# Band attention layers: the mask added to the scores by VectorE instead of by mask products on TensorE

## The chip, the core and the metric

The kernel runs on one core of a Trainium2 chip. The time is device time in microseconds of one execution; the shown time is the median of the runs. PE is TensorE (matmuls), PEld its weight loads, DVE VectorE, ACT ScalarE, POOL GpSimd, and SP the engine that issues most DMAs.

## The reference

The reference is a decoder with layer norms ahead of each part: a tensor x of 32 batch elements, 128 positions and 128 features goes through self-attention, cross-attention and feed-forward parts, eleven of them, and a last part named `L3_ffn`. The change lies in this last part. It holds six layers; each is a local attention with 16 heads of 64 features and a gated feed-forward:

```python
def local_attention(q, k, v):                      # windows of w = 32 positions
    ...                                            # keys and values of the window before and its own
    mask = (it < jb) | (it > jb + w) | (jb == -1)
    sim = jnp.einsum('bhwie,bhwje->bhwij', bq, bk2) * QK_SCALE      # 8.0
    sim = jnp.where(mask, -jnp.finfo(sim.dtype).max, sim)
    attn = jax.nn.softmax(sim, -1)
    out = jnp.einsum('bhwij,bhwje->bhwie', attn, bv2)
def attn_layer(x, Wqkv, qs, ksc, Wo):
    q, k, v = jnp.split(x @ Wqkv, 3, -1)           # then by heads
    q = l2norm(q) * qs
    k = l2norm(k) * ksc
    q = q * cos * scale + rotate_half(q) * sin * scale
    k = k * cos * inv + rotate_half(k) * sin * inv
    out = local_attention(q, k, v)
    return out @ Wo                                # 1024 features to 128
def ffn_layer(x, g, bln, W1, b1, W2, b2):
    hg = layer_norm(x, g, bln) @ W1 + b1
    a, gate = jnp.split(hg, 2, -1)
    return a * gelu(gate) @ W2 + b2
for i in range(6):
    x = attn_layer(shift_tokens(x), ...) + x
    x = ffn_layer(shift_tokens(x), ...) + x
```

A query at position i sees the keys at positions j with i - 32 <= j <= i: a band below the diagonal.

## The kernel before

The first 2770 us of the program are the other parts, which the change touches only through one constant tile. The last part is the method `l3_ffn` of class `Fast`. X, the stream Z and all work of a layer stay in SBUF; only the weights of the next layer are fetched while the present one runs.

**Work.** One unit of work n is one batch element in one layer: 6 x 32 = 192 units. The kernel doesn't cut the sequence into windows. It computes, for each head, the whole 128 x 128 matrix of scores, transposed (keys on partitions, queries along the free dimension), adds a mask of 0 inside the band and -1e30 outside, and takes the exponential, with no maximum subtracted since q and k are normalized. The sum of the exponentials comes out of the product with the values, through a column of ones in `va`.

**Steps of a unit**, with the tiles that they write:
- `queries(n, w)`: two products of 512 columns (the profile shows two rows for each fp32 product) into `qk`, 16 heads of 64 features; w=0 gives the queries, w=1 the keys.
- `squares`: ACT squares `qk` into `sq`. `swapped` and `rotated`: DVE multiplies `qk` by the two rotary tables `tab` into `rt` and `raw`; POOL adds them.
- `summed` and `scaled`: DVE sums the squares by head into `ss` and begins the inverse root; POOL finishes it and scales `raw`.
- `turned(n, us)`: TensorE transposes `raw` in four batches u=0..3 of four 128 x 128 tiles each into `rT`; ACT copies u=0 and 2, DVE u=1 and 3, into `qkT`.
- `scores(n)`: into two tiles `sc`, of eight heads each: first four mask products (an identity times `bandT`, 512 columns each, bfloat16), then 16 score products that add to them; ACT takes the exponential, scale 8, into `P`.
- `values`: the products of `P` with `va` into `av`; DVE takes the reciprocal of the sums `rs` and multiplies into `ao`. `features`: TensorE transposes `ao` (`oTp`), ACT copies to `oT`. `projected`: the product with `wo` into `y`, added to Z by DVE. `valued`: the product `vp` and its copy to `va`.
- Steps named `ff_...` and `shifted` work on four units at a time: the gated feed-forward (`gp`, `ap`, `u`, `fy`) and the shift of positions (`zT`, `zs`).

**Order.** The order is written out by hand. A loop over t runs a fixed list of steps, each for the unit t minus a lag:

```python
steps = ((features, 5), (summed, 1, 1), (scaled, 1), (queries, 0, 0), (squares, 0), (swapped, 0, 0),
         (rotated, 0, 0), (turned, 2, (0, 1)), (scores, 3), (summed, 0, 0), (turned, 2, (2, 3)),
         (queries, 0, 1), (squares, 0), (swapped, 0, 1), (rotated, 0, 1), (projected, 5), (values, 4))
blocks = ((ff_normed, 7), (ff_turn, 8), (ff_down, 11), (ff_up, 10), (ff_gates, 9), (ff_norm, 6))
```

The classes `Ordered` and `Lane` keep every engine to this order: each instruction of TensorE, VectorE, ScalarE and GpSimd is issued after the one before it on its engine. Each engine then runs ahead of the others only as far as its waits allow. Because all these instructions are recorded by `Lane`, the profile gives one line for them (L1342), and they are told apart by their tiles.

**PSUM.** Two pools share the eight banks. `p2` (function `banks`) has three buffers of two banks, used in turn by `qk`, `sc`, `sc`, `qk`, `av`, `av`, `vp`. `p1` (function `bank`) has two buffers of one bank, for `rT`, `oTp`, `y` and all small results. A tile that takes a buffer waits until the tile that had it before has been read.

Of the kernel before, what the change touches and what calls it, by code (L numbers as in the profile page):

```python
# [13 lines left out]
F32 = mybir.dt.float32  # L14
BF16 = mybir.dt.bfloat16
# [3 lines left out]
ALU = mybir.AluOpType  # L19
# [238 lines left out]
class General:  # L258
    def __init__(self, ctx, tc, i, out, names):
        self.tc, self.nc, self.i, self.out = tc, tc.nc, i, out  # L260
        nc = self.nc
        mats, cols, rows = names
        self.mat_at = {n: j for j, n in enumerate(mats)}
        self.col_at = {n: j for j, n in enumerate(cols)}
        self.row_at = {n: j for j, n in enumerate(rows)}
        cp = self.cp = ctx.enter_context(tc.tile_pool(name="const", bufs=1))
        self.X = cp.tile([128, NB, 128], F32, name="X")
        self.load_x()

        def load(key, dt=F32, eng=None):  # L270
            src = i[key]
            t = cp.tile(list(src.shape), dt, name=key)
            (eng or nc.scalar).dma_start(out=t, in_=src)
            return t

        self.half = load("c_half", BF16)
        self.small = load("c_small")
        self.cols = load("cols")
        self.rows = load("rows")
        self.big = load("c_big")  # L280
        self.ident = cp.tile([128, 128], F32, name="ident")
        make_identity(nc, self.ident)
        self.identh = cp.tile([128, 2, 128], BF16, name="identh")
        nc.vector.tensor_copy(self.identh[:, 0, :], self.ident)
        nc.vector.tensor_scalar(self.identh[:, 1, :], self.ident, 80.0, None, ALU.mult)
        self.ones = cp.tile([1, 128], F32, name="ones")
        nc.vector.memset(self.ones, 1.0)
        self.eps = cp.tile([128, 1], F32, name="eps")
        nc.vector.memset(self.eps, EPS)
        self.mv = cp.tile([128, NB, 2], F32, name="mv")  # L290
        self.rstd = cp.tile([128, NB], F32, name="rstd")
# [225 lines left out]
    def l0_ffn(self):  # L517
        nc, tc = self.nc, self.tc
        scale = 128.0 ** -0.5
        with ExitStack() as es:  # L520
            wk = es.enter_context(tc.tile_pool(name="L0f", bufs=2))
            one = es.enter_context(tc.tile_pool(name="L0f1", bufs=1))
            Z = one.tile([128, NB, 128], F32, name="Z")
            ss = one.tile([128, NB], F32, name="ss")
            self.rstds()
            for b4 in range(NB // 4):
# [18 lines left out]
                for j in range(4):  # L545
# [29 lines left out]
                    self.mm(y, aoT, self.mat("L0f_o"))  # L575
                    nc.vector.tensor_copy(Z[:, b, :], y)
                    self.sumsq(wk, ss[:, b:b + 1], y)
            self.l2scale(ss)
            ss2 = one.tile([128, NB], F32, name="ss2")
            for b4 in range(NB // 4):  # L580
                zT = self.trans4(wk, self.scaled4(wk, Z, ss, b4), "zT")
                for j in range(4):
                    b = 4 * b4 + j
                    y = self.p1([128, 128], "y")
                    self.mm(y, zT[:, 128 * j:128 * j + 128], self.mat("L0f_ff"))
                    nc.vector.tensor_copy(Z[:, b, :], y)
                    self.sumsq(wk, ss2[:, b:b + 1], y)
            self.l2scale(ss2)
            for b4 in range(NB // 4):
                z = self.scaled4(wk, Z, ss2, b4)  # L590
                nc.scalar.activation(z, z, AF.Gelu)
# [13 lines left out]

    def scaled4(self, wk, Z, ss, b4):
        z = wk.tile([128, 4, 128], F32, tag="zs", name="zs")
        for j in range(4):
            b = 4 * b4 + j
            self.nc.vector.tensor_scalar(z[:, j, :], Z[:, b, :], ss[:, b:b + 1], None, ALU.mult)  # L610
        return z
# [747 lines left out]
class Fast(General):  # L1359
# [6 lines left out]
    def __init__(self, *a):  # L1366
        super().__init__(*a)
        nc, cp = self.nc, self.cp
        self.cert = cp.tile([128, 2, 16], F32, name="cert")
        nc.vector.memset(self.cert, 1.0)  # L1370

        self.bandT = cp.tile([128, 4, 128], BF16, name="bandT")
        nc.gpsimd.memset(self.bandT, 0.0)
        for sign, base in ((1, 0), (-1, 32)):
            nc.gpsimd.affine_select(out=self.bandT, in_=self.bandT, pattern=[[0, 4], [sign, 128]],
                                    compare_op=ALU.is_ge, fill=-1.0e30, base=base, channel_multiplier=-sign)
        self.bandT = self.bandT.rearrange("p c q -> p (c q)")
        self.ncert = 0

    def all(self):  # L1380
# [428 lines left out]
    def l3_ffn(self):  # L1809
# [3 lines left out]
        nc = self.nc = Ordered(plain, tc)  # L1813
        N = DEPTH * NB
        with ExitStack() as es:
            one = es.enter_context(tc.tile_pool(name="L3f1", bufs=1))
# [4 lines left out]
            def mm(out, lhsT, rhs, start=True, stop=True):  # L1821
                nc.tensor.matmul(out, lhsT=lhsT, rhs=rhs, start=start, stop=stop)
# [7 lines left out]
            def banks(shape, name):  # L1830
                return p2.tile(shape, F32, tag="b", name=name)

            rot = one.tile([128, 256], F32, name="rot")
            nc.sync.dma_start(out=rot, in_=i["c_rot"].rearrange("s w c d -> s (w c d)"))
            Z = one.tile([128, NB, 128], F32, name="Z")
            zs2 = [one.tile([128, 4, 128], F32, name=f"zs{j}") for j in range(2)]
            va2 = [one.tile([128, 16, 65], F32, name=f"va{j}") for j in range(2)]
# [180 lines left out]
            def scores(n):  # L2018
                s = S[n]
                qkT = s["qkT"]  # L2020

                sc = [banks([128, 2, 4, 128], "sc") for _ in range(2)]
                for f in range(2):
                    for e in range(2):
                        mm(sc[f][:, e].rearrange("p c q -> p (c q)"), self.identh[:, 0, :], self.bandT, stop=False)
                s["P"] = []
                for f in range(2):
                    for c in range(4):
                        for e in range(2):
                            r = slice(64 * e, 64 * e + 64)  # L2030
                            mm(sc[f][:, e, c, :], qkT[r, 8 + 4 * f + c, :], qkT[r, 4 * f + c, :], start=False, stop=c == 3)
                    P = wk.tile([128, 8, 128], F32, tag="P", name="P", bufs=4)
                    nc.scalar.activation(P.rearrange("p h q -> p (h q)"), sc[f].rearrange("p e c q -> p (e c q)"), AF.Exp,
                                         scale=8.0)
                    s["P"].append(P)
# [96 lines left out]
            def ff_down(g):  # L2132
# [10 lines left out]
                if l == DEPTH - 1:  # L2143
# [4 lines left out]
            ahead = ((normed, 3), (x_values, 5), (x_scores, 6), (x_keys, 7), (x_turn, 8), (x_norm, 9), (x_root, 10))  # L2148
# [4 lines that stand above are left out]
# [906 lines left out]
```

## Time and profile before

| | us |
|---|---|
| median of 3 runs (lowest to highest) | 6221.49 (6221.09 to 6223.54) |
| the profiled execution | 6220.55 |
| its span, from the first to the last instruction | 6218.8 |
| busy in the span: PE | 5581.7 (90%) |
| PEld | 3944.6 (63%) |
| DVE | 4045.7 (65%) |
| POOL | 3086.2 (50%) |
| ACT | 2985.2 (48%) |
| mask products `sc<-bandT`: 768 rows of 0.379 (192 x 4) | first at 2806.5, last at 6158.6 |
| exponentials `P<-sc`: 384 rows, mean 1.022 | 372.4 |

The shares are averages over the whole program; the band layers fill the time from about 2770 to the end, and only they hold the instructions that change. Times of rows are microseconds from the span's start. A matmul's row is longer than the distance to the next one's start, because matmuls overlap; what a batch of them takes on PE is read from start to start.

### The profile page before, as it was taken

How to read it: one execution, taken by the hardware profiler on the slowest of the kernel's cores; microseconds unless marked ns; L12 is line 12 of the kernel's file. 1: busy time of each engine (PE TensorE's matmuls, PEld its weight loads, DVE VectorE, ACT ScalarE, POOL GpSimd, SP SyncE). 2: the span in 40 equal slices, each digit the busy share in tenths (PEclk: the TensorE clock that was granted, in tenths of full speed). 3: DMA queues.
4: the chain of work that ended last, by engine and by line, in shares of the span. 5: the costliest groups of instructions: out<-in, count | busy, mean ns of one | idle time of the engine just before them, and what ended most of it. 6: DMA issues, size and time to landing. Idle time of an engine off the chain costs nothing.

```text
span 6218.8 us, 137908 instructions
## 1 busy us (share of the span) xinstructions
PE 5581.7 (90%) x56611; PEld 3944.6 (63%) x56611; DVE 4045.7 (65%) x11609; ACT 2985.2 (48%) x4283; POOL 3086.2 (50%) x4833
## 2 busy tenths in 40 slices
PE   8967967777869999869999999999999999999998
PEld 4534546754546666646667767777777777766775
DVE  5576532345539999957666666666666676667664
ACT  5656621114425555524555545555555555554553
POOL 0041011011015555537666666666766667666773
PEclk9988976769989999989999999999999999999999
DMA  1000046543012222210000000000000000000000
GB/s 42 2 1 1 2 169 239 170 143 104 7 23 53 52 55 50 52 35 5 5 17 11 8 1 1 15 5 1 12 8 1 1 15 5 1 1 1 1 1 15
DMA packets 243263, 207.46 MB, mean 33 GB/s; under 512 B 125650, under 2 KB 230457, under 8 KB 237502
## 3 DMA queue, kind: packets, MB, share of 16 engines
q1 hardware_dynamic: 239164, 161.93, 9.1%
q0 software_dynamic: 2304, 33.56, 1.4%
q8 instruction: 447, 7.32, 0.5%
q10 hardware_dynamic: 1154, 3.06, 0.1%
q14 instruction: 194, 1.59, 0.1%
HBM read 140.57 MB, written 57.93 MB: 32 GB/s over the span
## 4 chain that ended last, share of the span: by engine, by line
PE 54%; DVE 10%; ACT 3%; issue 1%; POOL 1%; DMA 1%; SPq 1%; ACTq 0%; DVEq 0%; POOLq 0%
PE qk L1342 11%; PE sc L1342 8%; PE rT L1342 6%; PE vp L1342 6%; PE av L1342 5%; PE y L1342 5%; PE gp L1342 3%; PE oTp L1342 3%; PE fy L1342 2%; DVE rt L1342 1%; DVE raw L1342 1%; DVE ao L1342 1%; DVE neg L1342 1%; ACT sq L1342 1%; PE tp L1342 1%
## 5 line engine op out<-in xcount | busy, mean ns | idle before, releaser
L1342 POOL TENSOR_TENSOR raw<-raw,rt 128x1024 f32<-128x1024 f32 x384 | 902.9, 2357 | 335.9 <-DVE raw L1342 335.7
L1342 DVE TENSOR_TENSOR rt<-qk,tab 128x1024 f32<-128x1024 f32 x384 | 470.2, 1224 | 881.4 <-ACT sq L1342 862.4
L1342 POOL TENSOR_TENSOR raw<-raw,ry 128x2048 f32<-128x2048 f32 x224 | 811.3, 3622 | 17.6
L1342 PE MATMUL qk<-wqkv,zs 128*128 128x512 f32 x1536 | 727.6, 597 | 3.0 <-DVE zs L1342 3.0
L1342 ACT ACTIVATE sq<-qk 128x1024 f32<-128x1024 f32 x448 | 459.2, 1025 | 465.8 <-PE qk L1342 334.5
L1342 POOL TENSOR_TENSOR rt<-ry 128x32 f32<-128x32 f32 (+1 forms) x864 | 198.4, 230 | 751.1 <-DVE ry L1342 642.6
L1342 DVE TENSOR_REDUCE ss<-sq 128x16 f32<-128x1024 f32 x448 | 539.0, 1208 | 48.4 <-ACT sq L1342 47.1
L1342 DVE TENSOR_TENSOR raw<-qk,tab 128x1024 f32<-128x1024 f32 x384 | 466.1, 1214 | 0.0
L1342 ACT ACTIVATE P<-sc 128x1024 f32<-128x1024 f32 x384 | 372.4, 1022 | 187.7 <-PE sc L1342 187.2
L1342 ACT ACTIVATE PT<-sc 128x1024 f32<-128x1024 f32 x384 | 372.6, 1025 | 168.8 <-PE sc L1342 168.3
L1342 PEld LDWEIGHTS rT<-ident,raw 128*128 128x128 f32 x3072 | 342.0, 141 | 164.9 <-issue 65.8
L1342 PE MATMUL rT<-ident,raw 128*128 128x128 f32 x3072 | 433.5, 280 | 14.4 <-POOL raw L1342 6.1
L1342 ACT COPY va<-vp 128x1024 f32<-128x1024 f32 (+1 forms) x232 | 218.2, 941 | 453.3 <-PE vp L1342 453.1
L1342 PEld LDWEIGHTS y<-wo,oT 128*128 128x128 f32 x3072 | 372.8, 192 | 91.5 <-issue 78.7
L1342 PEld LDWEIGHTS sc<-qkT 64*128 64x128 f32 x6144 | 357.9, 188 | 81.4 <-issue 81.4
L1342 PE MATMUL av<-va,P 128*64 128x65 f32 x12288 | 400.9, 223 | 0.0
L1342 PE MATMUL sc<-qkT 64*128 64x128 f32 x6144 | 394.6, 278 | 0.0
L1342 PEld LDWEIGHTS av<-va,P 128*64 128x64 f32 x12288 | 374.3, 137 | 23.8 <-issue 0.8
L1342 PEld LDWEIGHTS qk<-wqkv,zs 128*128 128x128 f32 x1536 | 264.2, 192 | 192.1 <-issue 188.3
L1342 PE MATMUL y<-wo,oT 128*128 128x128 f32 x3072 | 374.4, 275 | 1.4 <-DVE qkT L1342 0.8
L1342 PE MATMUL vp<-wqkv,zs 128*128 128x512 f32 x768 | 362.9, 595 | 0.7 <-DVE rs L1342 0.7
L1342 POOL TENSOR_TENSOR X<-X,brep 128x512 f32<-128x512 f32 x24 | 30.5, 1271 | 548.5 <-DVE xn L1342 548.5
(425 smaller groups left out, 11609.2 us busy)
## 6 DMA issues: line engine op xcount, KB each, us to landing
rows<-scr SPq DMA_DIRECT2D x32, 672.0 KB
tup<-whole SPq DMA_DIRECT2D x8, 2048.0 KB
gt<-tup SPq DMA_DIRECT2D x64, 256.0 KB
tdn<-whole SPq DMA_DIRECT2D x8, 2048.0 KB
gd<-tdn SPq DMA_DIRECT2D x128, 128.0 KB
T<-flt SPq DMA_DIRECT2D x16, 1024.0 KB
wqkv<-in_dqkv SPq DMA_DIRECT2D x6, 1536.0 KB
scr<-dots SPq DMA_DIRECT2D x128, 66.0 KB
```

The costliest lines, as they stand in the source:

```text
L1342: self.last = call(*a, **k)
```

## The change

The mask moves from TensorE to VectorE. The constant `bandT` (bfloat16, 128 x 512, built at the program's start) and the four mask products of each unit go. A new constant `band` (fp32, 128 x 128) is built at the start of `l3_ffn`. The score products now write `sc` with nothing beneath them, all 16 of a unit first. Then, for each of the two halves, VectorE adds `band`, repeated for eight heads, to the 128 x 1024 scores in place in PSUM, and ScalarE's exponential follows.

```diff
-        self.bandT = cp.tile([128, 4, 128], BF16, name="bandT")
-        nc.gpsimd.memset(self.bandT, 0.0)
-        for sign, base in ((1, 0), (-1, 32)):
-            nc.gpsimd.affine_select(out=self.bandT, in_=self.bandT, pattern=[[0, 4], [sign, 128]],
-                                    compare_op=ALU.is_ge, fill=-1.0e30, base=base, channel_multiplier=-sign)
-        self.bandT = self.bandT.rearrange("p c q -> p (c q)")
...
+            band = one.tile([128, 128], F32, name="band")
+            nc.gpsimd.memset(band, 0.0)
+            for sign, base in ((1, 0), (-1, 32)):
+                nc.gpsimd.affine_select(out=band, in_=band, pattern=[[sign, 128]], compare_op=ALU.is_ge, fill=-1.0e30,
+                                        base=base, channel_multiplier=-sign)
...
                 sc = [banks([128, 2, 4, 128], "sc") for _ in range(2)]
-                for f in range(2):
-                    for e in range(2):
-                        mm(sc[f][:, e].rearrange("p c q -> p (c q)"), self.identh[:, 0, :], self.bandT, stop=False)
                 s["P"] = []
                 for f in range(2):
                     for c in range(4):
                         for e in range(2):
                             r = slice(64 * e, 64 * e + 64)
-                            mm(sc[f][:, e, c, :], qkT[r, 8 + 4 * f + c, :], qkT[r, 4 * f + c, :], start=False, stop=c == 3)
+                            mm(sc[f][:, e, c, :], qkT[r, 8 + 4 * f + c, :], qkT[r, 4 * f + c, :])
+                for f in range(2):
+                    h = sc[f].rearrange("p e c q -> p (e c) q")
+                    nc.vector.tensor_tensor(h, h, band.unsqueeze(1).to_broadcast([128, 8, 128]), ALU.add)
                     P = wk.tile([128, 8, 128], F32, tag="P", name="P", bufs=4)
                     nc.scalar.activation(P.rearrange("p h q -> p (h q)"), sc[f].rearrange("p e c q -> p (e c q)"), AF.Exp,
                                          scale=8.0)
```

## The prediction

> **What bounds the kernel now.** I read the page first (PE is busy 9 tenths or more from slice 20 on, the band layers), then the busy times by stretch, then the timelines of PE, DVE and ACT over one block, and last the waits, because a busy PE does not say whether less PE work would end sooner. A block is one pass of the loop over t; there are 6 x 32 = 192 that hold scores, in four kinds by the feed-forward work they carry: A (ff_up, ff_norm), B (ff_normed, ff_down), C (ff_turn, shifted), D (ff_gates). In the trace their w=0 query products start at 4404.45 (A), 4423.03 (B), 4440.55 (C), 4456.28 (D) and 4473.91 (next A): 18.58, 17.52, 15.73 and 17.63 us.
>
> The busy times by stretch; columns: stretch, its length, busy time (instructions) of PE, weight loads, DVE, ACT, POOL, granted clock, DMA share, GB/s. The third line is the four blocks.
>
> ```profile
> 200.00:320.00 120.00, 107.16 (x1388) 62.51 (x1386) 65.87 (x230) 85.89 (x111) 7.59 (x6) 1.00 0.01 2
> 2080.00:2120.00 40.00, 35.70 (x265) 27.68 (x261) 37.46 (x206) 21.45 (x36) 26.30 (x45) 0.91 0.15 36
> 4404.45:4473.91 69.46, 69.02 (x656) 49.07 (x655) 47.63 (x80) 35.49 (x49) 47.79 (x76) 1.00 0.01 2
> ```
>
> PE never rests for long in the blocks (69.02 of 69.46 us), DVE rests 21.83 us, or 5.46 a block. The PE timeline of block C (start, length, engine, line, operation, tiles, shapes, count):
>
> ```profile
> 4440.55 1.88 PE L1342 MATMUL qk<-wqkv,zs 128*128 128x512 f32 x4
> 4442.27 1.04 PE L1342 MATMUL rT<-ident,raw 128*128 128x128 f32 x8
> 4443.14 1.03 PE L1342 MATMUL sc<-bandT,identh 128*128 128x512 bf16 x4
> 4444.10 2.06 PE L1342 MATMUL sc<-qkT 64*128 64x128 f32 x32
> 4446.08 1.23 PE L1342 MATMUL rT<-ident,raw 128*128 128x128 f32 x8
> 4447.15 1.88 PE L1342 MATMUL qk<-wqkv,zs 128*128 128x512 f32 x4
> 4448.86 1.95 PE L1342 MATMUL y<-wo,oT 128*128 128x128 f32 x16
> ```
>
> The third row is what goes. Note the two rows of eight transposes: 1.04 us, then 1.23. The DVE timeline of the same block:
>
> ```profile
> 4443.64 1.23 DVE L1342 TENSOR_TENSOR rt<-qk,tab 128x1024 f32<-128x1024 f32 x1 [3.02 <-ACT sq L1342]
> 4444.78 1.21 DVE L1342 TENSOR_TENSOR raw<-qk,tab 128x1024 f32<-128x1024 f32 x1
> 4445.91 0.68 DVE L1342 COPY qkT<-rT 128x512 f32<-128x512 f32 x1
> 4446.51 1.21 DVE L1342 TENSOR_REDUCE ss<-sq 128x16 f32<-128x1024 f32 x1
> 4447.64 0.68 DVE L1342 COPY qkT<-rT 128x512 f32<-128x512 f32 x1
> 4450.24 1.23 DVE L1342 TENSOR_TENSOR rt<-qk,tab 128x1024 f32<-128x1024 f32 x1 [1.92 <-ACT sq L1342]
> ```
>
> The ACT timeline:
>
> ```profile
> 4442.52 1.02 ACT L1342 ACTIVATE sq<-qk 128x1024 f32<-128x1024 f32 x1 [0.65 <-ACT oT L1342]
> 4443.44 0.58 ACT L1342 COPY qkT<-rT 128x512 f32<-128x512 f32 x1
> 4445.31 1.94 ACT L1342 ACTIVATE P<-sc 128x1024 f32<-128x1024 f32 x2 [1.29 <-PE sc L1342]
> 4447.13 0.59 ACT L1342 COPY qkT<-rT 128x512 f32<-128x512 f32 x1
> 4449.11 1.02 ACT L1342 ACTIVATE sq<-qk 128x1024 f32<-128x1024 f32 x1 [1.39 <-PE qk L1342]
> ```
>
> And one row of the weight-load timeline, in block A:
>
> ```profile
> 4410.56 0.42 PEld L1342 LDWEIGHTS rT<-ident,raw 128*128 128x128 f32 x4 [0.15 <-DVE qkT L1342]
> ```
>
> The small pool has two buffers, so the fourth batch of transposes (u=3) can start only when DVE has copied out the second (u=1). That copy ends at 4409.82 + 0.68 = 4410.50 in block A, and the weights of u=3 load at 4410.56. So in the block's first part PE and the chain product, square (ACT), rt, raw, copy (DVE) are level: PE waits 0.15 us. I count from the w=0 product from here on. In block C the copy ends at 6.04 and u=3 starts at 6.10; the w=1 product starts at 6.60.
>
> **Removed: four mask products.** Four on PE per block, 4444.10 - 4443.14 = 0.96 us; 192 x 0.96 = 184 us of PE time. What of it is on the path? Without them PE does the products (1.72), the transposes u=0,1 (0.87), the scores (1.98) and u=2 (0.44), and stands at u=3 at 5.01. The copy of u=1 still ends at 6.04: nothing ahead of it on DVE or ACT waits for the mask products. u=3 starts at 6.10 as before and PE waits 1.09 us instead of 0.13. The gain in this place is zero, and the w=1 product stays at 6.60.
>
> The Trainium skill ("Perfetto Trace Analysis", Identifying the Most-Contended Engine) says to optimize first the engine with the highest occupancy, which speaks for taking work from PE. PE leads even if it is judged by its weight loads, as that section asks (49.07 us against DVE's 47.63). By the rule the sum would be the 184 us gained; by the row of block A it is nothing.
>
> **Added: two adds on DVE per block**, 128x1024, in place in PSUM with the band from SBUF. No row shows DVE writing PSUM. Nearest are rt and raw (PSUM and SBUF in, 1024 elements): 1.21 to 1.23 us, one start to the next 1.14; I take that. Below: a 512-element copy takes 0.60 from start to start and a 1024-element one 1.13, so 1024 elements at that slope are not under 1.06. Above: the 512-element scalar_tensor_tensor u is 7% slower than ao (0.74 against 0.69), so 1.22; far above, a pass each for reading and writing, 2.28. None of these can be a gain. 2 x 1.14 = 2.28 us fits into DVE's 5.46 idle us, so DVE is not the bound; its place is what counts. In the program's order they stand behind rt, raw and the copy of u=1, ahead of ss and the copy of u=3; the scores are done at 4.57, so the adds wait for their turn alone. On ACT the two exponentials now wait for them, and behind these in ACT's queue stand the copy of u=2 and the w=1 square. For u=2's copy waits y (projected): it takes the buffer that u=2 leaves.
>
> The walk in block C. DVE: copy of u=1 starts at 5.36, first add at 5.96, second 7.10, which ends at 8.32. ACT: second exponential at 8.35 (0.03 is the median from DVE's end to ACT's start), copy of u=2 0.90 later (as 4445.31 + 0.92 + 0.90 = 4447.13 shows) at 9.25, ending at 9.84; y at 9.90 with 0.05 for the semaphore. Before, y was at 8.31. **+1.58 us.** PE behind it (values, feed-forward, vp, oTp, next product) keeps its order; the score buffers come free at 9.37 with the second exponential, av asks for them at 11.78. DVE's tail moves less: the w=1 square starts at 9.73 (0.48 behind the copy's start, as the second oT copy behind the first) in place of 8.57, so rt, raw, Z, ao move by 1.16 and are not last. Blocks B and D go like C. In block A y gets the buffer of u=3, whose copy on DVE now ends at 10.05 (ss at 8.24, 1.13 later the copy, 0.68 long): y at 10.10, and with y 1.88, av 2.01 and four ap products 1.72 (as vp's four) PE would be at the third ap at 15.71. That one waits for u on DVE, which released it at 14.64 before and does so 1.16 later, 15.80. The later decides: **+1.16**.
>
> **Setup.** Three POOL operations leave the kernel's start (0.53 + 0.63 + 0.62 us) and three smaller ones go to the stage's start (by the rows of ident 0.20 + 2 x 0.28), ahead of the memsets of uc, zs and va; POOL idles 8.97 us there. I take zero, with -1.8 to +0.8. No DMA moves.
>
> **Sum.** Four blocks cost 3 x 1.58 + 1.16 = 5.90 more; 48 x 5.90 = 283 us. The profiled execution took 6220.55 (span 6218.80), so 6503.6; the median of the runs is 0.94 above it: **6505 us**. With adds of 1.06 and 1.22 the second add ends 0.16 earlier or later, 192 x 0.16 = 31 us: 6474 to 6536.
>
> **Rivals.**
> 1. *The clock drops* (slower still). PE's busy share would be (69.02 - 3.84) / 75.36 = 86%, with waits of 1.09 and about 1.6 us. The first two rows above, both 89% busy, stand for the two ends: clock 1.00 where the longest PE wait is 1.37 us, 0.91 where it is 2.51. I take 1.00, being nearer to 1.37. At 0.91 the PE part of a block (18.84 - 7.93 between 1.97 and 9.90, so 10.9 us) takes 1.08 more: 207 us, 6712. A tenth; any part of it is possible.
> 2. *The add in place takes two passes.* The second add then ends at 10.59 and y starts at 12.16, +3.85; block A +3.43 by DVE's tail: 48 x 14.98 = 719, 6221 + 719 = 6940. 5%.
> 3. *The adds sit in DVE's idle time and nothing comes later*: 6221, no change. It needs the copy of u=2 done by 8.26; ACT's order has it behind the exponentials. 2%.
> 4. *Faster.* The mask products' 0.96 us leave the path, 6221 - 184 = 6037. The place is the wait of u=3: it decides if the copy of u=1 ends by 5.09 or earlier in place of 6.04, and the adds stay off ACT's way. Against it: u=3 starts 0.06 us after that copy's end, the wait shown in block A. 4%.
>
> The Trainium skill ("TensorE: Matmul & The Clock Gate", Why this matters for your kernels) asks to avoid idle gaps of PE over about 3 us between matmul bursts; with 1.1 and 1.6 us the rule has no drop, and the sum stays 6505. The row with 0.91 and a longest wait of 2.51 us says that it can begin sooner, which makes up to 6712.
>
> **Numbers.** My case 0.79, rivals 0.10, 0.05, 0.02, 0.04. Range 6460 to 6630: the bounds of the add, and somewhat more than half of the clock's price. Left out are the two-pass case, the worst of the clock, and rivals 3 and 4. Faster by over 0.2% (12 us, about what a measurement can tell here) 0.04, within 0.02, slower 0.94.
>
> **What would show it.** No sc<-bandT; 384 rows sc<-sc,band of about 1.22 us on DVE, its busy time up by 470 us. From the w=0 to the w=1 product still 6.60 us, with PE idle before rT up by 0.96 x 192 = 184 us, released by DVE qkT. PE idle before y of about 1.6 us a block, by ACT qkT (in A by DVE qkT). Four blocks in about 75.4 us at a clock of 1.00. I am wrong at the first step if the w=1 product comes under 6.6 us, at the second if y starts near 8.3, and in size if the add's row is not near 1.22.

## The result, and the profile after

| | us |
|---|---|
| changed kernel, median of 4 runs (lowest to highest) | 6528.41 (6520.81 to 6530.94) |
| kernel before, same chip, median of 4 runs | 6221.29 (6219.01 to 6223.54) |
| ratio, 95% interval | 1.0489, 1.0477 to 1.0502 |
| the profiled execution after, and its span | 6530.52, 6528.7 |

The change made the kernel slower by 307 us, 23 us more than forecast and inside the range of 6460 to 6630. The lines below answer to those shown of the kernel before, from the same four blocks of the stage (A, B, C, D; the w=0 products now start at 4553.01, 4573.06, 4592.27 and 4609.70, the next A at 4629.03).

Busy times over the four blocks, columns as before:

```profile
4553.01:4629.03 76.02, 67.09 (x641) 47.23 (x640) 56.89 (x88) 35.54 (x49) 47.98 (x76) 1.00 0.01 1
```

The stretch is 76.02 us in place of 69.46. PE is idle 8.93 us in place of 0.44, and busy 1.93 us less. (Not 3.84 less: the scores now follow the transposes 0.97 us after their start, where the mask products followed after 0.87; in a batch a product of 0.28 us starts every 0.11, so that each of the two breaks that a block now has shows up to 0.17 more as busy; and y's batch has grown by 0.1.) DVE has 9.26 us more to do and is still idle for 19 us. The granted clock stays at 1.00, so this is waiting and not a slower engine. Where PE waits, the PE timeline of block C shows:

```profile
4594.95 2.06 PE L1342 MATMUL sc<-qkT 64*128 64x128 f32 x32
4598.37 0.66 PE L1342 MATMUL rT<-ident,raw 128*128 128x128 f32 x4 [0.78 <-DVE qkT L1342]
4598.86 1.88 PE L1342 MATMUL qk<-wqkv,zs 128*128 128x512 f32 x4
4602.17 2.05 PE L1342 MATMUL y<-wo,oT 128*128 128x128 f32 x16 [1.42 <-ACT qkT L1342]
```

No row of mask products stands ahead of the scores any more. From the w=0 to the w=1 product it is still 6.59 us (4598.86 - 4592.27): what the removed 0.96 us left free has become the wait before the transposes of u=3. Then y starts 9.90 us into the block, where it was 8.31. DVE and ACT in the same block:

```profile
4597.63 0.68 DVE L1342 COPY qkT<-rT 128x512 f32<-128x512 f32 x1
4598.23 2.35 DVE L1342 TENSOR_TENSOR sc<-sc,band 128x1024 f32<-128x1024 f32 x2
4600.49 1.21 DVE L1342 TENSOR_REDUCE ss<-sq 128x16 f32<-128x1024 f32 x1
```

```profile
4599.49 2.16 ACT L1342 ACTIVATE P<-sc 128x1024 f32<-128x1024 f32 x2 [3.75 <-DVE sc L1342]
4601.54 0.58 ACT L1342 COPY qkT<-rT 128x512 f32<-128x512 f32 x1
4602.01 1.04 ACT L1342 ACTIVATE sq<-qk 128x1024 f32<-128x1024 f32 x1
```

The chain reads downward: the two adds end at 4600.58, the exponentials at 4601.65, the copy of u=2 at 4602.12, and y starts 0.05 us after that. The lists of waits and of costliest groups give the same over the whole run (waits: us in total, times, longest):

```profile
PEld rT L1342 <- DVE qkT L1342: 191.3, 189, 2.2
PEld y L1342 <- ACT qkT L1342: 320.3, 142, 2.3
PEld y L1342 <- DVE qkT L1342: 112.5, 47, 2.4
```

In the kernel before, the list has no row for the second, and for the first and third:

```profile
PEld rT L1342 <- DVE qkT L1342: 10.3, 43, 2.2
PEld y L1342 <- DVE qkT L1342: 11.8, 46, 1.0
```

And the adds:

```profile
L1342 DVE TENSOR_TENSOR sc<-sc,band 128x1024 f32<-128x1024 f32 x384 | 452.0, 1223 | 1.8 <-PE sc L1342 1.8
```

The growth of the first wait from 10.3 to 191.3 us is not like for like: the list leaves out waits of up to 0.15 us, and before the change three blocks in four lie there. Taken block by block, the weight loads of u=3 stood 0.15 us before (0.08 in B) and 1.01 after (0.94 in B), so the removal added 0.865 us a block to the wait, 192 x 0.865 = 166 us. An add takes 1.223 us.

### The profile page after: what moved, and what is told of

It is laid out like the page before. It is cut to its first block, busy times and chain, and to the rows that moved or that the text cites. A ratio compares the mean times of both kernels' runs of the same rounds, so it can differ in the third digit from the quotient of the medians.

```text
span 6528.7 us, 136757 instructions
## 1 busy us (share of the span) xinstructions
PE 5481.1 (84%) x55843; PEld 3853.1 (59%) x55843; DVE 4484.9 (69%) x11993; ACT 2989.6 (46%) x4283; POOL 3094.2 (47%) x4833
## 5 line engine op out<-in xcount | busy, mean ns | idle before, releaser
L1342 ACT ACTIVATE P<-sc 128x1024 f32<-128x1024 f32 x384 | 393.3, 1024 | 673.3 <-DVE sc L1342 652.8
L1342 PE MATMUL y<-wo,oT 128*128 128x128 f32 x3072 | 393.8, 281 | 277.6 <-ACT qkT L1342 202.8
L1342 PEld LDWEIGHTS y<-wo,oT 128*128 128x128 f32 x3072 | 357.4, 191 | 433.1 <-ACT qkT L1342 320.3
L1342 PE MATMUL rT<-ident,raw 128*128 128x128 f32 x3072 | 452.8, 280 | 157.2 <-DVE qkT L1342 146.5
L1342 PEld LDWEIGHTS rT<-ident,raw 128*128 128x128 f32 x3072 | 341.8, 141 | 327.1 <-DVE qkT L1342 191.3
L1342 DVE TENSOR_TENSOR sc<-sc,band 128x1024 f32<-128x1024 f32 x384 | 452.0, 1223 | 1.8 <-PE sc L1342 1.8
```

The lines of the kernel that those rows point to most:

```text
L1342: self.last = call(*a, **k)
```

## Experiments

**The theory.** PE has two appointments in a band block. Before u=3's transposes it waits for DVE's copy of u=1, so that less PE work ahead of them is worth nothing; y then waits for the copy that frees its buffer, and the adds delay that copy through ACT's queue. The loss is the adds' place, not their 452 us. **The rivals:** PE time counts as such (and the gain is hidden in a larger loss); or DVE's added work, its load or its PSUM traffic, is the price wherever it stands. Ratios below are to the kernel before, run beside each on the same chip. There its medians were 6227 to 6229 us, so the ratio is what carries over to the 6221 above, and microseconds "over the kernel before" are against the run beside it. Positions in a block are medians over the blocks of a kind, counted from the w=0 product, in the trace.

### e1_no_mask: the removal alone

This kernel leaves the mask out altogether.

```diff
                 for f in range(2):
-                    h = sc[f].rearrange("p e c q -> p (e c) q")
-                    nc.vector.tensor_tensor(h, h, band.unsqueeze(1).to_broadcast([128, 8, 128]), ALU.add)
...
-                                         scale=8.0)
+                                         scale=1.0e-6)
```

> The changed kernel without its two DVE adds in each band block; the mask products stay away too, so the mask is left out of the computation (the exponential's scale is set to 1e-6 so that the sums stay finite). This leaves the removal alone. My theory (PE waits before the transposes of u=3 for DVE's copy of u=1 whatever it has left out, and the second exponential starts as before): first weights of y back at 8.3 us in the block, four blocks back at 69.5 us, in all about 6221 us (6213 to 6230). The rival, that TensorE's time is the bound and the removed products' 0.96 us in each of 192 blocks are gained: about 6037 us, y at about 7.4.

Measured: ratio 0.9998 (0.9988 to 1.0007). y is back at 8.31, the four kinds of block take 18.58, 17.51, 15.74 and 17.63 us as before, to the hundredth. PE's wait before u=3 is that of the changed kernel:

```profile
PEld rT L1342 <- DVE qkT L1342: 190.9, 189, 1.9
```

Taking 0.96 us of work out of each of 192 blocks from the engine that is busy 99% of the time gained nothing.

### e2_both_masks: the adds alone

```diff
+                for f in range(2):
+                    for e in range(2):
+                        mm(sc[f][:, e].rearrange("p c q -> p (c q)"), self.identh[:, 0, :], self.bandT, stop=False)
...
-                            mm(sc[f][:, e, c, :], qkT[r, 8 + 4 * f + c, :], qkT[r, 4 * f + c, :])
+                            mm(sc[f][:, e, c, :], qkT[r, 8 + 4 * f + c, :], qkT[r, 4 * f + c, :], start=False, stop=c == 3)
```

> The changed kernel with the four mask products on TensorE put back and the two DVE adds kept, so that the mask is added twice. This leaves the addition alone. My theory (the products lie in PE's wait for u=1's copy, the adds alone set when y may start): the time of the changed kernel, about 6528 us (6520 to 6540), with PE's wait before u=3's transposes about 0.96 us shorter per block than in the changed kernel. The rival, in which PE's time counts and the changed kernel has kept its gain of 184 us inside a larger loss: about 6712 us.

Measured: ratio 1.0488 (1.0470 to 1.0505), the changed kernel's 1.0489. The blocks take the changed kernel's times to the hundredth; PE's wait before u=3 falls from 191.3 to 9.3 us, since the products fill it:

```profile
PEld rT L1342 <- DVE qkT L1342: 9.3, 36, 2.2
```

With e1 this splits the change cleanly: the removal is worth nothing, the adds all of the loss. The rival with PE time is out at both ends.

### e3_copy_first: the adds where they are, the copy of u=2 out of their way

Here and below, `turned` for u=2,3 is split: `third` emits the transposes and ACT's copy of u=2, `fourth` DVE's copy of u=3; `masked` is one add with its exponential, and `scores` keeps the score products.

```diff
-  (turned, 2, (0, 1)), (scores, 3), (summed, 0, 0), (turned, 2, (2, 3)),
-  (queries, 0, 1), (squares, 0), ...
+  (turned, 2, (0, 1)), (scores, 3), (third, 2), (masked, 3, 0), (masked, 3, 1),
+  (summed, 0, 0), (fourth, 2), (queries, 0, 1), (squares, 0), ...
```

> The changed kernel, with ACT's copy of u=2 issued ahead of the two exponentials instead of behind them; the adds, the exponentials and all else stay. My theory (the adds cost because the copy that y waits for stands in ACT's queue behind the second exponential, which waits for the second add): y back at 8.3 us or earlier; DVE's remaining work of the block ends about 0.7 us later than in the kernel before, which the blocks of kind C pay with 0.3 and those of kind A with 0.7, B and D with nothing: 6221 + 48 x 1.0 = about 6269 us (6235 to 6310). The rival, in which the adds cost by DVE's load or by reading and writing PSUM beside PE: stays at about 6528 us.

Measured: ratio 1.0126 (1.0109 to 1.0143), 80 us over the kernel before in place of 307. Same adds, same DVE and PE work; only ACT's copy has changed places, and y is back at 8.31, as in this block C, whose w=0 product starts at 4491.35:

```profile
4499.66 1.95 PE L1342 MATMUL y<-wo,oT 128*128 128x128 f32 x16
```

That is the place of the loss. The expectation of 48 us was too low by some 30, though the range held it. The ACT timeline of the same block and the list of waits say why:

```profile
4500.89 1.02 ACT L1342 ACTIVATE sq<-qk 128x1024 f32<-128x1024 f32 x1 [0.17 <-DVE ss L1342]
```

```profile
ACT sq L1342 <- DVE ss L1342: 46.4, 192, 4.5
```

ACT's second squares write the buffer that DVE's `ss` reads, and `ss` now stands behind both adds. I had followed ACT's queue but not this buffer. Blocks C took 0.63, blocks A 0.99 and blocks D 0.06 us more than before (0.3, 0.7 and nothing expected).

### e7_second_add_late: that step mended

```diff
-  (masked, 3, 0), (masked, 3, 1), (summed, 0, 0), (fourth, 2), (queries, 0, 1), (squares, 0), ...
+  (masked, 3, 0), (summed, 0, 0), (queries, 0, 1), (squares, 0), (masked, 3, 1), (fourth, 2), ...
```

> e3_copy_first with one thing more: the second add and its exponential stand behind the second half's query projection and squares (so DVE sums the first half's squares after one add, not after two). e3_copy_first came out 39 us longer than I had expected because ACT's second squares waited for that sum: 0.24 us per block in the list of waits, squares at 9.55 us in the block instead of 9.27. My theory: squares at 8.56 again, DVE's following product at 9.97 instead of 9.69 in the kernel before, which only the blocks of kind A pay: about 13 us over the kernel before (5 to 30 over), ratio 1.002. The rival, that e3_copy_first's excess is DVE's two added instructions themselves, wherever they stand: 60 to 80 us over the kernel before, ratio 1.010 to 1.013.

Measured: ratio 1.0021 (1.0011 to 1.0030), 14 us over. B, C and D take their old times to the hundredth, A 18.84 in place of 18.58. So DVE does both adds in every block, 384 in all, for 14 us instead of 307. The rival that DVE's work or its PSUM traffic has a price of its own is out, up to these 14 us, of which 48 x 0.26 = 12.5 are the blocks A.

### e8_second_group and e9_first_group: one add of the two

```diff
+                for f in (0,):        # e9_first_group: (1,)
+                    for e in range(2):
+                        mm(sc[f][:, e].rearrange("p c q -> p (c q)"), self.identh[:, 0, :], self.bandT, stop=False)
...
+                    if f == 1:        # e9_first_group: f == 0
                         nc.vector.tensor_tensor(h, h, band.unsqueeze(1).to_broadcast([128, 8, 128]), ALU.add)
```

> Half the change: DVE adds the mask to the second group of heads only, the first group keeps its two mask products on TensorE. My theory (what counts is when the second exponential may start): the first exponential runs at 4.8 us as before, the one add ends at 7.2, the second exponential at 8.2, u=2's copy at 8.7, y at 8.8 instead of 8.3; blocks B, C, D +0.58 each with the 0.11 of a stalled y, A +0.26: 48 x 2.0 = about 96 us over the kernel before (80 to 115), ratio 1.0155. The rival, a price in proportion to DVE's adds: half of 307, 154 us, ratio 1.025, the same as for e9_first_group.

> The other half of the change: DVE adds the mask to the first group of heads only, the second group keeps its two products on TensorE. My theory: the first exponential waits for the add until 7.2 us, the second stands behind it until 9.2 although its scores are ready, u=2's copy ends at 9.7, y at 9.7; B, C, D +1.5 each, A +1.0: 48 x 5.5 = about 265 us over the kernel before (235 to 285), ratio 1.043: one add of the two costs nearly all. The rival, a price in proportion to DVE's adds: 154 us, ratio 1.025, the same as for e8_second_group.

Measured: the second group alone 1.0134 (1.0117 to 1.0151), 83 us, with y at 8.77 as expected. The first group alone 1.0242 (1.0225 to 1.0259), 150 us: not my 265, and by its size the proportional rival's 154. But the two halves differ, which that rival excludes, and the trace of e9_first_group shows another reason. Its PE, DVE and ACT timelines in a block C:

```profile
4522.32 2.05 PE L1342 MATMUL y<-wo,oT 128*128 128x128 f32 x16 [0.48 <-DVE qkT L1342]
```

```profile
4521.59 0.68 DVE L1342 COPY qkT<-rT 128x512 f32<-128x512 f32 x1
```

```profile
4522.41 0.59 ACT L1342 COPY qkT<-rT 128x512 f32<-128x512 f32 x1
```

y starts 0.05 us after DVE's copy of u=3, while ACT's copy of u=2 has not even begun. In this program y was given the other buffer of the small pool: its weight loads wait for DVE's copy in 189 blocks and for ACT's in none, where the changed kernel has 47 and 142. Within one program all blocks of a kind behave alike; the block A of the prediction was such a case, here all blocks are. What decides the choice is not shown: the list of steps is the same in both. I had taken the changed kernel's assignment over without looking it up.

### e11_first_group_u2: the same single add, y in the buffer of u=2

```diff
-  (queries, 0, 1), (squares, 0), (swapped, 0, 1), (rotated, 0, 1), ...
+  (queries, 0, 1), (squares, 0), (swapped, 0, 1), (fourth, 2), (rotated, 0, 1), ...
```

> e9_first_group with DVE's copy of u=3 behind the next rt product instead of ahead of it, so that y is given the buffer of u=2, not that of u=3. In e9_first_group y started at 8.96 us in the block, 0.06 after u=3's copy on DVE, and while u=2's copy on ACT ran until 9.64: it had been given the other buffer than in the changed kernel, which my expectation had not seen. My theory (the buffer that y is given decides what one add costs): y at 9.70, blocks B, C, D +1.5, A +1.5 by DVE's later tail, 48 x 6.0 = about 290 us over the kernel before (260 to 310), ratio 1.0465, with one add of the two. The rival (price in proportion to DVE's adds, or 150 us as in e9_first_group whatever buffer y takes): ratio 1.024.

Measured: ratio 1.0454 (1.0437 to 1.0472), 282 us over, with one add of the two. The PE timeline of a block C, and ACT's copy:

```profile
4594.66 2.05 PE L1342 MATMUL y<-wo,oT 128*128 128x128 f32 x16 [1.21 <-ACT qkT L1342]
```

```profile
4594.01 0.59 ACT L1342 COPY qkT<-rT 128x512 f32<-128x512 f32 x1
```

y is at 9.69 and waits for ACT's copy of u=2. In blocks B, C and D, where y's start is what lengthens the block, it is 0.73 us later than in e9_first_group and the blocks are 0.73 to 0.74 us longer; A is 0.59 longer. So a single add costs 83, 150 or 282 us, depending on which copy it holds up and whether y waits for that copy.

### e5_reordered, e6_reordered_products, e10_products_exp_early: both appointments moved

e5_reordered also moves the next block's u=0,1 transposes and copies ahead of DVE's `swapped` and `rotated`, so that u=3's transposes find their buffer free:

```diff
-  (queries, 0, 0), (squares, 0), (swapped, 0, 0), (rotated, 0, 0), (turned, 2, (0, 1)), (scores, 3),
-  (summed, 0, 0), (turned, 2, (2, 3)), (queries, 0, 1), (squares, 0), ...
+  (queries, 0, 0), (squares, 0), (turned, 2, (0, 1)), (swapped, 0, 0), (rotated, 0, 0), (scores, 3),
+  (third, 2), (masked, 3, 0), (summed, 0, 0), (queries, 0, 1), (squares, 0), (masked, 3, 1), (fourth, 2), ...
```

e6_reordered_products is that order with the mask on TensorE (`masked` is then the exponential alone). e10_products_exp_early has `(masked, 3, 0)` ahead of `(third, 2)`.

> The changed kernel with its order of work changed: the transposes of the next block's u=0 and u=1 and their copies stand ahead of the gate products of DVE (swapped, rotated), so that u=3's transposes no longer wait for u=1's copy; ACT's copy of u=2 stands ahead of the exponentials; the second add stands behind the second half's work on the queries. My theory (both waits that hold PE in a band block are gone, and with them the 0.96 us of mask products become worth their time): second query projection at about 5.8 us in the block instead of 6.6, y at about 7.5; against the kernel before four blocks about 2.0 us shorter, in all about 6126 us (6080 to 6200), under the kernel before. The rival, in which DVE's added 2.4 us per block are themselves the cost: at or above 6400 us.

> The kernel before, its mask products on TensorE, with exactly the new order of e5_reordered (only the adds are missing from it). This shows what TensorE's mask products are worth once nothing but TensorE holds the block. My theory: the order gives back part of PE's waits, but the products fill them: four blocks 0.8 us shorter than in the kernel before, about 38 us under it (25 to 60 under), that is ratio 0.994; and e5_reordered stays some 50 us under this one, so that with this order the same change of the mask gains about 0.8% where it lost 4.9%. The rival, that the gain of e5_reordered came from the order alone: this kernel is as fast as e5_reordered, ratio 0.985 or less.

> e6_reordered_products (mask products on TensorE, new order) with its first exponential ahead of ACT's copy of u=2 instead of behind it. In e6_reordered_products the blocks A were 0.48 us longer than in the kernel before, since an unnamed ACT instruction of 1.29 us that stands ahead of the block's first exponential there had moved in front of the second squares (9.05 us in the block instead of 8.43). My theory: squares at 8.43 in A too, blocks A back to 18.5, four blocks 0.4 us shorter than before: about 19 us under the kernel before (5 to 30 under), ratio 0.997; then the products cost this order about 70 us against e5_reordered's adds. The rival, that the product version can reach e5_reordered's time by a better place for the exponential: ratio 0.985 to 0.990.

Measured: e5_reordered 0.9853 (0.9837 to 0.9870), 90 us under the kernel before; e6_reordered_products 1.0012 (1.0002 to 1.0022), 5 us over where 38 under was expected; e10_products_exp_early 0.9955 (0.9938 to 0.9972), 30 us under. The miss lies partly in the blocks A: the ACT timeline of one in e6_reordered_products shows

```profile
4549.58 1.28 ACT L1342 ACT_TABLE_LOAD   x1
4550.88 1.02 ACT L1342 ACTIVATE P<-sc 128x1024 f32<-128x1024 f32 x1
4551.80 1.02 ACT L1342 ACTIVATE sq<-qk 128x1024 f32<-128x1024 f32 x1
```

a load of 1.28 us that sits ahead of the first exponential in the blocks A and had moved in front of the squares. With the exponential early, A went from 19.06 to 18.46. For the rest I had over-estimated the order: B, C and D gained only 0.06, 0.13 and 0.13 us over the kernel before.

e5_reordered beats both kernels. Against e6_reordered_products, which has exactly its order, the adds gain 1.6%, so the order alone is not the gain; against e10_products_exp_early, the better of the two with the mask on TensorE, about 1.0%. The four blocks of the one and of the other (e5_reordered first):

```profile
4372.89:4440.57 67.68, 66.39 (x640) 47.80 (x639) 56.30 (x88) 36.29 (x49) 47.80 (x75) 1.00 0.01 2
```

```profile
4393.85:4462.86 69.01, 68.57 (x657) 49.16 (x655) 47.65 (x80) 35.91 (x49) 47.82 (x75) 1.00 0.01 2
```

PE is busy 98% of the first stretch although DVE has 8.65 us more to do than in the second. Of the 3.84 us of mask products, 1.33 reach the end. The transposes of u=3, which now wait for nothing, start 0.86 us earlier than in e10_products_exp_early (5.16 against 6.03), not 0.96. The w=1 product follows them by 0.44 in that trace, which would be 5.60 here; it starts at 5.80, 0.05 us after DVE's `raw` ends, as in this block C from 4408.31:

```profile
4412.84 1.22 DVE L1342 TENSOR_TENSOR raw<-qk,tab 128x1024 f32<-128x1024 f32 x1
4414.11 1.98 PE L1342 MATMUL qk<-wqkv,zs 128*128 128x512 f32 x4
```

At y 0.56 us are left (7.62 against 8.18). Blocks B and D keep them, C keeps 0.28, and A is 0.07 longer: there PE waits 1.08 us before the third `ap` product for DVE's u (0.4 in e10_products_exp_early). So DVE's chain comes due next, up to `raw` in every block and at its tail in A; in C PE waits 0.3 us for DVE's Z.

## Why the prediction was right, point by point

1. **"The gain in this place is zero, and the w=1 product stays at 6.60."** It stayed at 6.60 in blocks A, C and D and at 6.53 in B, as before. e1_no_mask shows the zero by itself. The size of the wait was off: PE would have been at u=3 at 5.16, not 5.01 (that is where u=3 starts in e5_reordered, the earlier batches starting at the same times), so the wait is 0.94 us in place of 1.09, and it grew by 0.86 us a block, 166 us in all, in place of 184. The scores start at 2.69, 0.10 later than 3.55 - 0.96; why, no run shows. It cost the forecast nothing, because the wait ends with DVE's copy either way. "Perfetto Trace Analysis", Identifying the Most-Contended Engine, in the Trainium skill would have optimized PE first; the 184 us that the prediction worked out by it did not come while PE had an appointment to wait for. The row of 0.15 us before u=3 was the one that decided.
2. **The walk, +1.58 in B, C, D.** Every point of it came within 0.01 us: second add ends 8.32, second exponential 8.35, copy of u=2 ends 9.85, y 9.91 (forecast 8.32, 8.35, 9.84, 9.90). The blocks got longer by 1.69 to 1.70. The missing 0.11 is, but for 0.01, y's own batch: from y to av 1.98 us in place of 1.88. In the trace before, y's first weights load at 7.89, 0.43 us ahead of its first product, and products follow every 0.11 us; after the wait they load with the first product, and the second product comes 0.21 later. In blocks C, before and after:

```profile
4448.44 0.19 PEld L1342 LDWEIGHTS y<-wo,oT 128*128 128x128 f32 x1 [0.24 <-issue]
```

```profile
4602.17 1.86 PEld L1342 LDWEIGHTS y<-wo,oT 128*128 128x128 f32 x16 [2.25 <-ACT qkT L1342]
```

   0.11 x 144 = 16 us.
3. **Block A, +1.16.** Measured +1.47. The mis-sized term is "released it at 14.64 before and does so 1.16 later": DVE's u did not start at the end of DVE's own tail (13.84 + 1.18 = 15.02), but at 15.26, because PE had come late to the first ap product (12.21 before, 14.09 now) and u waits for it; its two rows end at 15.22. I had let DVE hold PE and not PE hold DVE. The third ap is at 16.06, not 15.80. The block A shown in the prediction (from 4404.45), then the one after (from 4553.01):

```profile
4416.66 1.98 PE L1342 MATMUL ap<-xT,w 128*128 128x512 f32 x4
4418.29 1.40 DVE L1342 SCALAR_TENSOR_TENSOR u<-ap,cols,g 128x512 f32<-128x512 f32 x2
4419.09 1.09 PE L1342 MATMUL ap<-xT,w 128*85 128x512 f32 x2 [0.44 <-DVE u L1342]
```

```profile
4567.11 3.06 PE L1342 MATMUL ap<-xT,w 128*128 128x512 f32 x6
4568.27 1.61 DVE L1342 SCALAR_TENSOR_TENSOR u<-ap,cols,g 128x512 f32<-128x512 f32 x2
```

   0.31 x 48 = 15 us.
4. **The sum.** 283 + 16 + 15 = 314, against 303 us measured in the band layers of the two profiled executions (the first eight blocks lengthened by 5.3 us together, where eight later ones mostly do by 13.1). A further 6.8 lie ahead of the first band block. That point falls anywhere from 2768 to 2778 us in the twelve profiled executions of this study, so I do not count it to the change. So errors of opposite sign partly cancelled, which is luck; and nothing of what the forecast missed is the clock, for whose price the upper part of the range had been left.
5. **The rivals.** *Clock:* 1.00 from 2860 to 6440 us of the span (0.86 and 0.90 in the short stretches at the two ends of the band layers, where the kernel before has 0.85 and 0.88), with PE 88% busy and the weight loads' waits of 1.02 and 2.25 us a block in C, so its 207 us are out. The Trainium skill's rule on gaps over about 3 us ("TensorE: Matmul & The Clock Gate", Why this matters for your kernels) had no drop here, and there was none. *Two passes:* 1.223 us an add, next to rt's 1.23. *Hidden:* false in this order, and true to 14 us in e7_second_add_late, by the condition that the prediction gave (the copy of u=2 done by 8.26). *Faster:* its condition (u=1's copy early, the adds off ACT's way) is what e5_reordered makes, and there about a third of the 184 us appears (1.33 x 48 = 64, against e10_products_exp_early).
6. DVE's busy time rose by 439 us, not the 470 named: 384 rows of 1.223 us do sum to 470, but the two of a unit overlap (2.35 us together), so that they cover 452, and part of that overlaps the neighbouring rows.

## What to carry to other kernels

Before counting work that is taken from the busiest engine, find the next point where that engine waits, however short the wait; until that point moves, the work only lengthens the wait. For work given to an idle engine ask who stands behind its consumer in the next queue and which buffer those hold: here the same two adds cost 307, 80 or 14 us, or helped to gain 90, by order alone. Which buffer a tile is given can differ from one program to the next: look it up for each variant, since an assignment taken over from another variant cost one of my expectations 115 us.

## What the runs showed of the hardware

- A DVE add in place in PSUM, 128x1024 f32 with the second operand broadcast from SBUF, takes 1.223 us, as much as one that reads PSUM and writes SBUF (rt 1.23, raw 1.21).
- A batch of y that starts after a wait took 0.10 us more than one that follows PE's own work (1.98 against 1.88): its first weights load with the first product and not 0.43 us ahead, and the first step is 0.21 in place of 0.11 us.
- PE waits of 0.78 and of 1.42 to 1.61 us in every block, at 88% busy, left the granted clock at 1.00.
- Taking 0.96 us of mask products out of PE's stream brought what follows forward by only 0.86 us (scores at 2.69 in place of 3.55).
- A table load on ACT (ACT_TABLE_LOAD) took 1.28 us. In e6_reordered_products, where it stood ahead of a square that DVE waited for, blocks A took 0.60 us more than in e10_products_exp_early, where it did not.
